# A recommender on one core: the product with W2 moves from TensorE to ScalarE, and the columns are marked anew every 16 blocks of items

## The chip, the cores and the metric

The kernel runs on one core of a Trainium2 chip. The metric is the time of one execution in device microseconds. The kernel before takes 43372.13 us in the median of three runs (43352.09 to 43403.7).

## The reference, cut to what matters

There are 50001 items with 32 neighbours each, and 16384 users with a history of 100 items and one target item.

```python
def _neighbor_attn(E, near_full):
    V = E[near_full]                                  # items x 32 x 32
    scores = einsum('nd,nkd->nk', E, V) / sqrt(32)
    return einsum('nk,nkd->nd', softmax(scores), V)

a_sus, a_inf = _neighbor_attn(E_in, near), _neighbor_attn(E_out, near)
h = concat([E_hist[history], a_sus[history], a_inf[history]])   # users x 100 x 128
t = concat([E_tgt[target], a_inf[target], a_sus[target]])       # users x 128
x = h * t[:, None, :]
z = relu(einsum('bld,hd->blh', x, W1) + b1)           # W1: 128 x 128
scores = einsum('blh,h->bl', z, W2[0])                # W2: 1 x 128
exp_A = exp(scores) * ((history != target) & (history != 0))
attn = exp_A / sqrt(sum(exp_A))
s = sum(h * attn)                                     # one number for all
pred = cosine(s * ones, t);  return sigmoid(pred)
```

## The kernel before, in words

The **item stage** builds the table of h rows (129 numbers: the sum of a row, and the row). It runs over 391 blocks of 128 items. For each block GpSimd (POOL) issues 26 indirect gathers, one for each of 26 neighbours (`gather`, L169). The other six neighbours of every item are read as columns of `cols`, a bf16 copy of the whole embedding table that stays in SBUF: `run` loads an address into a register and copies one column, 352 of the 768 by a TensorE matmul with the identity (L239), 248 by ScalarE (L235), 168 by VectorE (L237). `turn` (L264) brings the columns back into rows. VectorE then does scores, maximum, weighted sums (`scores`, `attended`), ScalarE the Exp.

The **user stage** takes 128 blocks of 128 users each; below "user" means such a block. A user has five chunks of 20 history positions, 640 chunks in all. For chunk s, POOL gathers 20 rows per user (`gather`, L534) into one of HB = 3 row buffers. VectorE (DVE) forms x = h * t (L548), copies the row sums out (`hsum`, L554) and turns x in blocks of 32 x 32 (L562) into one of XB = 2 buffers `xb`. SP writes it to DRAM in four pieces (L576) and reads it back with features on partitions (`xT`, L582). TensorE (PE) multiplies by W1 in five matmuls of 512 columns (`hidden`, L589), ScalarE (ACT) does relu over pairs of them (`relu`, L603) from two PSUM buffers. The product with W2 is again a matmul: `scored` (L613) multiplies each 128 x 512 z by `pick`, a matrix with W2 in one of 32 columns, so that the 25 matmuls of a user lay their results into 25 rows of one PSUM tile `bank`. When the 25th is done, DVE turns the bank (`weights`, `flat`, L621) and four DMAs carry it to `score`; then come Exp (L635) and the masked sums (L641 to L644).

The order is written by hand: each engine takes its instructions in the order of the loop over s. Three links matter below. The copy `hsum` of chunk s waits for the first W1 matmul of chunk s - XB (`after(copy, first.pop(s - XB))`). The gathers of chunk s wait for the `hsum` of chunk s - HB, which frees their row buffer. And `flat` stands in DVE's queue one step after the user's last chunk, ahead of the x of the next chunk. Scored matmuls run LS = 4 behind the hidden ones, in alternation with them.

Of the kernel before, what the change touches and what calls it, by code (L numbers as in the profile page):

```python
# [13 lines left out]
E = mybir.EngineType  # L14
# [36 lines left out]
W = 1 + D  # L51
M = 2
HB = 3
XB = 2
ZB = 4
LS = 4

# [8 lines left out]
Q_ACT = {6: 248}  # L66
TURN = P * NF

@with_exitstack
def kernel(
# [41 lines left out]
    with (  # L114
# [7 lines left out]
    ):  # L122
        cols = n_c.tile([P, 3, C], BF16, name="cols")
        its = {}
        subs = {}
# [85 lines left out]
        def run(s, who, q0, n):  # L211
            it, j = divmod(s, NSUB)
            u = subs[s]
            k, i = divmod(q0, P)
            k += j * NF + NF - fetched(s)
# [12 lines left out]
            for q, value in enumerate(found):  # L228
# [9 lines left out]
                else:  # L238
                    nc.tensor.matmul(pc[:, :, q : q + 1], identb, of, start=True, stop=True)  # L239

        def pieces(who, q0, q1):
# [15 lines left out]
        def turn(s):  # L257
            u = subs[s]
            fb = u.pop("fb")
            nf = fetched(s)  # L260
# [114 lines left out]
        for s in range(NT + 3):  # L375
# [11 lines left out]
            if f is not None:  # L387
                nf = fetched(f)
                subs[f]["fb"] = n_s.tile([P, 3, P * NF], BF16, name="fb", bufs=2)
# [58 lines left out]
    w1T = const.tile([D, HID], F32, name="w1T")  # L448
    pick = const.tile([HID, NG, GS], F32, name="pick")
    num = const.tile([P, UC], F32, name="num")  # L450
# [18 lines left out]

    rows = ring("h", HB, LQ, W)  # L470
    xs = ring("x", 2, LQ, D)
    xbs = ring("xb", XB, Q, LQ, GS)
    xTs = ring("xT", 3, Q * LQ * GS)
    zr = ring("z", ZB, 2, COLS)
    hists = {}
# [5 lines left out]
    with (  # L481
        tc.manual_schedule(engines={E.PE, E.Activation, E.DVE, E.SP, E.Pool}),
        tc.tile_pool(name="u_s", bufs=3) as u_s,
        tc.tile_pool(name="ps_r", bufs=2, space=bass.MemoryType.PSUM) as ps_r,
        tc.tile_pool(name="ps_t", bufs=2, space=bass.MemoryType.PSUM) as ps_t,
        tc.tile_pool(name="ps_s", bufs=2, space=bass.MemoryType.PSUM) as ps_s,
    ):
        users = {}
        landed, went, turned, moved, hid, zs = {}, {}, {}, {}, {}, {}
        bank, first, second, third = {}, {}, {}, {}  # L490

# [38 lines left out]
        def gather(s):  # L530
            c, k = divmod(s, NCH)
            for q in range(LQ):
                l = k * LQ + q
                landed[s, q] = nc.gpsimd.indirect_dma_start(  # L534
# [3 lines left out]
                    in_offset=bass.IndirectOffsetOnAxis(  # L538
                        ap=users[c]["hidx"][:, l : l + 1], axis=0
                    ),  # L540
                )

        def blocks(s):
            c, k = divmod(s, NCH)
            u = users[c]
            h = rows[s % HB]
            x = xs[s % 2]
            made = nc.vector.tensor_tensor(  # L548
                x,
                h[:, :, 1:W],  # L550
                u["tp"].to_broadcast([P, LQ, D]),
                ALU.mult,
            )
            copy = nc.vector.tensor_copy(  # L554
                u["hsum"][:, k * LQ : (k + 1) * LQ], h[:, :, 0:1].rearrange("p q o -> p (q o)")
            )
            for q in range(LQ - 1):
                gone = landed.pop((s, q))
# [3 lines left out]
            turn = nc.vector.transpose(  # L562
                xb.rearrange("p b q j -> p q b j"), x.rearrange("p q (b i) -> p q b i", b=Q)
            )
            if s >= XB:
                after(copy, first.pop(s - XB))
# [4 lines left out]

        def move(s):
            xb = turned.pop(s)
            there = theres[s % XB]
            for a in range(Q):
                one = nc.sync.dma_start(  # L576
                    there[:, :, a, :].rearrange("b i n -> i b n"),
                    xb[a * GS : (a + 1) * GS].rearrange("p b q j -> p b (q j)"),
                )
                went.setdefault(s, []).append(one)  # L580
            xT = xTs[s % 3]
            nc.sync.dma_start(xT, there.rearrange("b i a n -> (b i) (a n)"))  # L582
            moved[s] = xT

        def hidden(n):
            s, m = divmod(n, PER)
            if n % 2 == 0:
                hid[n // 2] = ps_r.tile([HID, 2, COLS], F32, name="z_ps")
            one = nc.tensor.matmul(  # L589
                hid[n // 2][:, n % 2, :],  # L590
                w1T,
                moved[s][:, m * COLS : (m + 1) * COLS],
                start=True,
                stop=True,
            )
            if m == 0:
                first[s] = one
            if m == PER - 1:
                moved.pop(s)

        def relu(pair):
            zs[pair] = zr[pair % ZB]
            second[pair] = nc.scalar.activation(zs[pair], hid.pop(pair), AF.Relu, bias=b1_sb)  # L603
            if pair >= ZB:
                covered(second[pair], second.pop(pair - ZB))
                covered(second[pair], third.pop(2 * (pair - ZB)))
                covered(second[pair], third.pop(2 * (pair - ZB) + 1))

        def scored(n):
            c, g = divmod(n, NG)  # L610
            if g == 0:
                bank[c] = ps_s.tile([GS, COLS], F32, name="bank")
            third[n] = nc.tensor.matmul(  # L613
                bank[c], pick[:, g, :], zs[n // 2][:, n % 2, :], start=g == 0, stop=g == NG - 1
            )
            if n % 2 == 1:
                zs.pop(n // 2)

        def weights(c):
            flat = u_t.tile([GS, COLS], F32, name="flat", bufs=2)  # L620
# [4 lines left out]
            of = flat[:, 0 : Q * L].rearrange("p (k a q) -> p k a q", k=NCH, a=Q)  # L625
            for a in range(Q):
                nc.sync.dma_start(
                    score[a * GS : (a + 1) * GS, :].rearrange("p (k q) -> p k q", k=NCH), of[:, :, a, :]
                )
            users[c]["score"] = score  # L630
# [15 lines left out]
        USERS = UC  # L646
        last = USERS * NCH
        groups = USERS * NG
        nc.sync.dma_start(tidx, target.rearrange("(p c) -> p c", p=P))
# [7 lines left out]
        nc.vector.tensor_copy(tidf, tidx)  # L657
        nc.vector.memset(pick, 0.0)
        for g in range(NG):
            nc.vector.tensor_copy(pick[:, g, g : g + 1], w2_sb)  # L660
# [4 lines left out]
        for s in range(last + 3):  # L665
            c, k = divmod(s, NCH)
            if s < last:
                if k == 0 and c % BSUB == 2 and 0 < c // BSUB and c // BSUB + 1 < UC // BSUB:
                    history_of(c // BSUB + 1)
# [5 lines left out]
                if k == 3 and c + 1 < USERS:  # L675
                    target_work(c + 1)
            for m in range(PER):
                n = s * PER + m
                if n < groups:
                    hidden(n)  # L680
                    if n % 2 == 1:
                        relu(n // 2)
                if 0 <= n - LS < groups:
                    scored(n - LS)
            done, left = divmod(s - NCH, NCH)
            if 0 <= done < USERS and left == 1:
                weights(done)
            if 0 <= done < USERS and left == 2:
                summed(done, ended(done))

# [78 lines left out]
```

## Time and profile before

| | |
|---|---|
| median of three runs | 43372.13 us |
| profiled execution, its span | 43228.8 us |
| span to median | 143.3 us |
| item stage | 0 to 24304 us |
| user stage | 24305 us to the end |
| busy share of the span: POOL, PE, DVE, ACT | 50%, 34%, 33%, 29% |
| DMA queues' share of 16 engines, hardware and software | 13.3%, 12.1% |

The profiled execution's own time is its span; what a run takes beside it is the 143.3 us. The busy shares are a mean over two stages. In the 40 slices of the page POOL stands at 3 to 4 tenths in the item stage and at 6 in the user stage, PE at 2 and then 4, ACT at 3 to 4 and then 0 to 1. TensorE's granted clock is full in the item stage and 6 to 7 tenths in the user stage.

### The profile page before, as it was taken

How to read it: one execution, taken by the hardware profiler on the slowest of the kernel's cores; microseconds unless marked ns; L12 is line 12 of the kernel's file. 1: busy time of each engine (PE TensorE's matmuls, PEld its weight loads, DVE VectorE, ACT ScalarE, POOL GpSimd, SP SyncE). 2: the span in 40 equal slices, each digit the busy share in tenths (PEclk: the TensorE clock that was granted, in tenths of full speed). 3: DMA queues.
4: the chain of work that ended last, by engine and by line, in shares of the span. 5: the costliest groups of instructions: out<-in, count | busy, mean ns of one | idle time of the engine just before them, and what ended most of it. 6: DMA issues, size and time to landing. Idle time of an engine off the chain costs nothing.

```text
span 43228.8 us, 542122 instructions
## 1 busy us (share of the span) xinstructions
PE 14536.1 (34%) x156212; PEld 6850.6 (16%) x156212; DVE 14230.3 (33%) x72584; ACT 12567.9 (29%) x102055; POOL 21816.3 (50%) x23124
## 2 busy tenths in 40 slices
PE   2222222222222222222222344444444444444444
PEld 1222222222222222222222100000000000000000
DVE  3444444444444444444444322222222222222222
ACT  3444444444444444444444201001010100000011
POOL 4334333343433334334343566666666666666665
PEclk9999999999999999999999867767666767677676
DMA  2000000000000000000000244444444444444444
GB/s 67 18 18 19 18 19 18 18 19 18 19 18 19 18 18 19 18 18 19 18 19 19 74 130 139 136 133 140 134 135 140 133 133 139 131 133 141 130 133 132
DMA packets 1617140, 3049.96 MB, mean 71 GB/s; under 512 B 739104, under 2 KB 831328, under 8 KB 1531840
## 3 DMA queue, kind: packets, MB, share of 16 engines
q1 hardware_dynamic: 874368, 1826.09, 13.3%
q0 software_dynamic: 739776, 1189.19, 12.1%
q8 instruction: 1238, 20.28, 0.2%
q14 instruction: 1758, 14.40, 0.1%
HBM read 2110.12 MB, written 909.58 MB: 70 GB/s over the span
## 4 chain that ended last, share of the span: by engine, by line
another core or an unknown queue 36%; issue 24%; ACT 16%; PE 9%; DVE 5%; DMA 5%; POOL 2%; ACTq 1%; SPq 1%; DVEq 0%; POOLq 0%
ACT fb L235 13%; PE pc L239 3%; PE z_ps L589 3%; DMA xT<-there 2%; POOL h L534 2%; DVE x L548 2%; PE bank L613 2%; PE rows L264 2%; DMA there<-xb 1%; ACTq L216 1%; DVE xb L562 1%; ACT z L603 1%; DVE fb L237 1%; SPq L576 1%
## 5 line engine op out<-in xcount | busy, mean ns | idle before, releaser
L169 POOL DMA_INDIRECT v<-in_egeo_dram,nidx x10190 | 9616.4, 944 | 14607.6 <-DVE tot L336 11594.1
L534 POOL DMA_INDIRECT h<-table,hidx x12800 | 12078.5, 944 | 6582.5 <-issue 3946.8
L235 ACT COPY fb<-cols 128x3 bf16 x95976 | 9824.6, 201 | 737.3 <-issue 680.8
L239 PE MATMUL pc<-cols,identb 128*128 x136224 | 5147.4, 168 | 14104.4 <-issue 13853.8
L589 PE MATMUL z_ps<-xT,w1T 128*128 128x512 f32 x6400 | 4632.4, 813 | 10706.5 <-DMA xT<-there 3875.3
L237 DVE COPY fb<-cols 128x3 bf16 x65016 | 5526.7, 167 | 4501.3 <-issue 4438.6
L239 PEld LDWEIGHTS <-identb 128*128 128x128 bf16 x136224 | 4442.4, 104 | 14783.8 <-issue 14782.3
L603 ACT ACTIVATE z<-z_ps,b_sb 128x1024 f32<-128x1024 f32 x1600 | 1775.3, 1113 | 17042.8 <-remote 7924.7
L613 PE MATMUL bank<-z,pick 128*32 128x512 f32 x6400 | 3979.7, 709 | 0.0
L275 ACT COPY v<-rows 128x384 f32<-128x384 f32 x387 | 185.0, 478 | 12603.5 <-PE rows L264 6318.7
L589 PEld LDWEIGHTS z_ps<-xT,w1T 128*128 128x128 f32 x6400 | 1208.6, 236 | 14036.0 <-issue 8731.7
L283 DVE COPY_PREDICATED v<-odd,rows 128x384 f32<-128x384 int32 x387 | 225.2, 582 | 9227.4 <-ACT v L275 9227.4
L621 DVE STREAM_TRANSPOSE flat<-bank 32x512 f32<-32x512 f32 x128 | 132.0, 1032 | 9028.3 <-remote 7940.9
L264 PE MATMUL rows<-identb,fb 128*128 128x128 bf16 x6966 | 1135.4, 297 | 3656.1 <-issue 3643.2
L548 DVE TENSOR_TENSOR x<-h,tp 128x2560 f32<-128x2560 f32 x640 | 1793.3, 2802 | 1099.1 <-DMA h<-table,hidx 650.4
L562 DVE STREAM_TRANSPOSE xb<-x 128x2560 f32<-128x2560 f32 x640 | 1819.6, 2843 | 0.0
L330 DVE TENSOR_TENSOR pw<-v,small 128x1024 f32<-128x1024 f32 x782 | 1423.1, 1900 | 46.7 <-ACT small L294 45.3
L264 PEld LDWEIGHTS <-fb 128*128 128x128 bf16 x6966 | 708.5, 132 | 4113.9 <-issue 4103.2
L641 DVE TENSOR_TENSOR ea<-ea,keep 128x100 f32<-128x100 f32 x128 | 33.6, 263 | 3543.3 <-ACT ea L635 2802.8
L613 PEld LDWEIGHTS bank<-z,pick 128*32 128x32 f32 x6400 | 478.6, 117 | 3204.1 <-issue 3202.6
L306 DVE TENSOR_REDUCE sc<-pw 128x64 f32<-128x2048 f32 x391 | 894.5, 2288 | 20.3 <-remote 6.9
L299 DVE TENSOR_TENSOR pw<-v,small 128x2048 f32<-128x2048 f32 x391 | 894.3, 2287 | 16.7 <-DVE v L283 1.9
(73 smaller groups left out, 3200.5 us busy)
## 6 DMA issues: line engine op xcount, KB each, us to landing
there<-xb SPq DMA_DIRECT2D x2560, 320.0 KB
xT<-there SPq DMA_DIRECT2D x640, 1280.0 KB
h<-table,hidx POOLq DMA_INDIRECT x12800
v<-in_egeo_dram,nidx POOLq DMA_INDIRECT x10190
table<-row SPq DMA_DIRECT2D x391, 64.5 KB
cols<-parts SPq DMA_DIRECT2D x1, 18768.0 KB
parts<-fb SPq DMA_DIRECT2D x32, 576.0 KB
own<-in_egeo_dram SPq DMA_DIRECT2D x391, 32.0 KB
```

The costliest lines, as they stand in the source:

```text
L169: nc.gpsimd.indirect_dma_start(out=v[:, k].rearrange("p t d -> p (t d)"), out_offset=None, in_=egeo, in_offset=bass.IndirectOffsetOnAxis(a ...
L235: nc.scalar.copy(to, of)
L237: nc.vector.tensor_copy(to, of)
L239: nc.tensor.matmul(pc[:, :, q : q + 1], identb, of, start=True, stop=True)
L264: nc.tensor.matmul(got[:, k].rearrange("p h d -> p (h d)"), fb[:, a, k * P : (k + 1) * P], identb, start=a == 0, stop=a == 2,)
L330: nc.vector.tensor_tensor(wv[:, t].rearrange("p d k -> p k d"), u["v"][:, :, t, :], u["sm"][:, 2 + t, :].rearrange("p (k o) -> p k o", o=1 ...
L534: landed[s, q] = nc.gpsimd.indirect_dma_start(out=rows[s % HB][:, q, :], out_offset=None, in_=table, in_offset=bass.IndirectOffsetOnAxis(a ...
L548: made = nc.vector.tensor_tensor(x, h[:, :, 1:W], u["tp"].to_broadcast([P, LQ, D]), ALU.mult,)
L562: turn = nc.vector.transpose(xb.rearrange("p b q j -> p q b j"), x.rearrange("p q (b i) -> p q b i", b=Q))
L589: one = nc.tensor.matmul(hid[n // 2][:, n % 2, :], w1T, moved[s][:, m * COLS : (m + 1) * COLS], start=True, stop=True,)
L603: second[pair] = nc.scalar.activation(zs[pair], hid.pop(pair), AF.Relu, bias=b1_sb)
L613: third[n] = nc.tensor.matmul(bank[c], pick[:, g, :], zs[n // 2][:, n % 2, :], start=g == 0, stop=g == NG - 1)
```

## The change

The user stage no longer has the `scored` matmuls, `pick`, and the turn of the bank on DVE. After the relu (now 128 x 1536 from `za` and 128 x 1024 from `zb`, one PSUM buffer each), ACT multiplies all 128 x 2560 of z by W2, one factor per partition. DVE turns that in blocks of 32 x 32 into `zT` and sums each run of 32, two chunks after the chunk itself (`partial`, LAG = 2). Once per user one matmul with `fold` adds the four quarters, and ACT copies the bank out. Rings change: row buffers 3 to 5, `xb` and the DRAM buffers 2 to 3, x 2 to 1, z from four of 1024 to three of 2560. The last user's last chunk of 20 is cut into 12 and 8. The first gather of each of the last two users waits for DVE's turn of the chunk before (CALM).

In the item stage `again` copies one column of `cols` onto itself on DVE before every 16th block, which therefore stands behind all earlier readers of `cols` and before all later ones; the identity for the column matmuls is copied anew at the same place. This happens 24 times.

```diff
+        def again(s):
+            it, j = divmod(s, NSUB)
+            _, found = nc.values_load_multi_w_load_instructions(
...
+            one = cols[:, :, ds((value - base) // 2, 1)]
+            nc.vector.tensor_copy(one, one)
...
+                if e not in idbs:
+                    again(f)
+                    idbs[e] = n_s.tile([P, P], BF16, name="idb", bufs=2)
+                    nc.vector.tensor_copy(idbs[e], ident)
...
+            if k == 0 and c >= UC - CALM:
+                after(landed[s, 0], turns[s - 1])
...
+        def hidden(s):
+            per = chunks[s][3] * P // COLS
+            xT = moved.pop(s)
+            z = zr[s % ZB]
+            for lo, hi, name in ((0, min(FIRST, per), "za"), (FIRST, per, "zb")):
...
+                z_ps = ps_r.tile([HID, PER - FIRST if lo else FIRST, COLS], F32, name=name)
+                for m in range(lo, hi):
+                    one = nc.tensor.matmul(
...
+                nc.scalar.activation(
+                    z[:, lo * COLS : hi * COLS],
+                    z_ps[:, 0 : hi - lo].rearrange("h m n -> h (m n)"),
+                    AF.Relu,
+                    bias=b1_sb,
+                )
+            nc.scalar.activation(z[:, 0 : per * COLS], z[:, 0 : per * COLS], AF.Copy, scale=w2_sb)
+
+        def partial(s):
...
+            nc.vector.transpose(
+                zT[:, 0 : Q * n].rearrange("p x i -> p (x i)"), zr[s % ZB][:, 0 : n * P]
+            )
+            nc.vector.tensor_reduce(
+                parts[c][:, :, q0 : q0 + n],
+                zT[:, 0 : Q * n].rearrange("p (a q) i -> p a q i", a=Q),
+                AX.X,
+                ALU.add,
+            )
+
+        def folded(c):
+            bank = ps_s.tile([GS, Q * L], F32, name="bank")
+            nc.tensor.matmul(
+                bank, fold, parts.pop(c).rearrange("p a l -> p (a l)"), start=True, stop=True
+            )
...
-            nc.vector.transpose(
-                flat.rearrange("p (g n) -> p n g", g=GS), bank.pop(c).rearrange("p (n j) -> p n j", j=GS)
-            )
+            nc.scalar.copy(flat.rearrange("p a l -> p (a l)"), users[c]["bank"])
```

How the order on PE changes, in the middle of the user stage. Before, a hidden matmul and a scored one alternate; names with a number are ring buffers:

```order
L613 MATMUL bank<-z_940047,pick 32x512
L589 MATMUL z_ps<-xT_940046,w1T 128x512
L613 MATMUL bank<-z_940047,pick 32x512
L589 MATMUL z_ps<-xT_940046,w1T 128x512
L613 MATMUL bank<-z_940048,pick 32x512
L589 MATMUL z_ps<-xT_940044,w1T 128x512
```

The same engine in the changed kernel, one user from fold to fold:

```order
L665 MATMUL bank<-part,fold 32x400
L633 MATMUL za<-xT_940191,w1T 128x512 x3
L633 MATMUL zb<-xT_940191,w1T 128x512 x2
L633 MATMUL za<-xT_940192,w1T 128x512 x3
L633 MATMUL zb<-xT_940192,w1T 128x512 x2
L633 MATMUL za<-xT_940190,w1T 128x512 x3
L633 MATMUL zb<-xT_940190,w1T 128x512 x2
L633 MATMUL za<-xT_940191,w1T 128x512 x3
L633 MATMUL zb<-xT_940191,w1T 128x512 x2
L633 MATMUL za<-xT_940192,w1T 128x512 x3
L633 MATMUL zb<-xT_940192,w1T 128x512 x2
L665 MATMUL bank<-part,fold 32x400
```

A user has 26 matmuls on PE where it had 50. On DVE before, around the end of a user, the turn of the bank stands between the chunks:

```order
L554 COPY hsum<-h_940038 128x20
L562 STREAM_TRANSPOSE xb_940043<-x_940041 128x20x4x32
L621 STREAM_TRANSPOSE flat<-bank 32x16x32
L548 TENSOR_TENSOR x_940040<-h_940039,tp 128x2560
L554 COPY hsum<-h_940039 128x20
L562 STREAM_TRANSPOSE xb_940042<-x_940040 128x20x4x32
L641 TENSOR_TENSOR ea<-ea,keep 128x100
```

On DVE in the changed kernel every chunk has a turn and a sum for the chunk two back:

```order
L587 COPY hsum<-h_940182 128x20
L595 STREAM_TRANSPOSE xb_940189<-x_940186 128x20x4x32
L653 STREAM_TRANSPOSE zT_940196<-z_940193 128x2560
L656 TENSOR_REDUCE part<-zT_940196 128x4x20
L581 TENSOR_TENSOR x_940186<-h_940183,tp 128x2560
L587 COPY hsum<-h_940183 128x20
L595 STREAM_TRANSPOSE xb_940187<-x_940186 128x20x4x32
```

The wait for PE's bank has gone from DVE's queue; a wait for ACT's scaled z of two chunks before stands in every chunk instead.

## Rows read from the trace of the kernel before

**Rows 1.** Head of the page.

```profile
span 43228.8 us, 542122 instructions
```

**Rows 2.** Busy time by windows, 2000 us of the user stage; first line names the columns.

```profile
core 0: us, PE busy (x) PEld busy (x) DVE busy (x) ACT busy (x) POOL busy (x), PEclk, DMA share, GB/s
34000.00:36000.00 2000.00, 872.32 (x1364) 179.24 (x1364) 427.24 (x332) 196.81 (x225) 1291.38 (x1369) 0.70 0.47 137
```

**Rows 3.** Timeline of POOL, user stage: start, duration, operation, idle time before it.

```profile
24304.95 0.94 POOL L504 DMA_INDIRECT t<-ttab,tidx  x1 [79.67 <-DMA table<-row]
...
30042.77 0.94 POOL L534 DMA_INDIRECT h<-table,hidx  x1 [14.93 <-DVE hsum L554]
30044.02 0.95 POOL L534 DMA_INDIRECT h<-table,hidx  x1 [0.30 <-issue]
...
30066.49 0.94 POOL L534 DMA_INDIRECT h<-table,hidx  x1 [0.30 <-issue]
...
30073.17 0.94 POOL L534 DMA_INDIRECT h<-table,hidx  x1 [4.49 <-DVE hsum L554]
...
43124.45 0.94 POOL L534 DMA_INDIRECT h<-table,hidx  x1 [0.30 <-issue]
```

**Rows 4.** Waits from 26000 to 42000 us: total us, times, longest.

```profile
DVE flat L621 <- remote: 6959.4, 97, 75.0
...
POOL h L534 <- DVE hsum L554: 2242.8, 201, 26.5
```

**Rows 5.** Timeline of DVE around one user's end.

```profile
30072.84 2.85 DVE L562 STREAM_TRANSPOSE xb<-x 128x2560 f32<-128x2560 f32 x1
...
30184.35 1.03 DVE L621 STREAM_TRANSPOSE flat<-bank 32x512 f32<-32x512 f32 x1 [65.75 <-remote]
```

**Rows 6.** Timeline of ACT in POOL's first long run of gathers.

```profile
24388.59 1.11 ACT L603 ACTIVATE z<-z_ps,b_sb 128x1024 f32<-128x1024 f32 x1 [7.35 <-remote]
24410.99 1.11 ACT L603 ACTIVATE z<-z_ps,b_sb 128x1024 f32<-128x1024 f32 x1 [21.29 <-remote]
...
24522.99 1.11 ACT L603 ACTIVATE z<-z_ps,b_sb 128x1024 f32<-128x1024 f32 x1 [21.29 <-remote]
24546.09 1.11 ACT L603 ACTIVATE z<-z_ps,b_sb 128x1024 f32<-128x1024 f32 x1 [21.99 <-remote]
```

**Rows 7.** Busy time by windows in the item stage, POOL idle and POOL gathering.

```profile
12014.00:12044.00 30.00, 10.19 (x300) 8.99 (x300) 18.94 (x135) 22.60 (x212) 1.17 (x2) 1.00 0.04 10
...
12056.00:12066.00 10.00, 1.00 (x6) 0.52 (x5) 0.52 (x3) 0.00 (x0) 7.56 (x9) 1.00 0.15 26
```

**Rows 8.** Timeline of POOL late in its first long run.

```profile
24540.07 1.09 POOL L534 DMA_INDIRECT h<-table,hidx  x1 [0.30 <-issue]
...
24549.87 0.94 POOL L534 DMA_INDIRECT h<-table,hidx  x1 [0.30 <-issue]
```

**Rows 9.** Costliest groups of the page: busy us, mean ns; idle before.

```profile
L589 PE MATMUL z_ps<-xT,w1T 128*128 128x512 f32 x6400 | 4632.4, 813 | 10706.5 <-DMA xT<-there 3875.3
L603 ACT ACTIVATE z<-z_ps,b_sb 128x1024 f32<-128x1024 f32 x1600 | 1775.3, 1113 | 17042.8 <-remote 7924.7
L613 PE MATMUL bank<-z,pick 128*32 128x512 f32 x6400 | 3979.7, 709 | 0.0
...
L562 DVE STREAM_TRANSPOSE xb<-x 128x2560 f32<-128x2560 f32 x640 | 1819.6, 2843 | 0.0
...
L306 DVE TENSOR_REDUCE sc<-pw 128x64 f32<-128x2048 f32 x391 | 894.5, 2288 | 20.3 <-remote 6.9
```

**Rows 10.** Timeline at the border between two item blocks.

```profile
12038.83 3.26 ACT L235 COPY fb<-cols 128x3 bf16 x32
...
12040.53 3.66 DVE L330 TENSOR_TENSOR pw<-v,small 128x1024 f32<-128x1024 f32 x2
12040.70 1.03 PE L239 MATMUL pc<-cols,identb 128*128 x32 [1.56 <-issue]
```

**Rows 11.** Timeline of the tail: SP and PE after the last chunk's turn.

```profile
43140.02 3.43 SPq L576 DMA_DIRECT2D there<-xb  x4
...
43152.78 2.08 PE L589 MATMUL z_ps<-xT,w1T 128*128 128x512 f32 x2 [7.04 <-DMA xT<-there]
```

More of the change, by code (lines that the diff above doesn't have):

```diff
@@ L51 @@
 W = 1 + D
[L52 to L56, printed above, removed]
+HB = 5
+XB = 3
+ZB = 3
+LAG = 2
+CALM = 2
+ENDING = (20, 20, 20, 20, 12, 8)
+FIRST = 3
 BF16 = mybir.dt.bfloat16
@@ L530, in gather @@
         def gather(s):
-            c, k = divmod(s, NCH)
-            for q in range(LQ):
-                l = k * LQ + q
+            c, k, q0, n = chunks[s]
+            for q in range(n):
                 landed[s, q] = nc.gpsimd.indirect_dma_start(
@@ L554, in blocks @@
             copy = nc.vector.tensor_copy(
[L555 removed]
+                u["hsum"][:, q0 : q0 + n], h[:, 0:n, 0:1].rearrange("p q o -> p (q o)")
             )
[L557 removed]
+            for q in range(n - 1):
                 gone = landed.pop((s, q))
@@ L581, in move @@
             xT = xTs[s % 3]
-            nc.sync.dma_start(xT, there.rearrange("b i a n -> (b i) (a n)"))
+            nc.sync.dma_start(
+                xT[:, 0 : Q * n * GS].rearrange("p (a n) -> p a n", a=Q),
+                there[:, :, :, 0 : n * GS].rearrange("b i a n -> (b i) a n"),
+            )
             moved[s] = xT
[L585 to L594, printed above, removed]
-            )
[L596 to L614, printed above, removed]
-            )
-            if n % 2 == 1:
-                zs.pop(n // 2)
+        def hidden(s):
[3 more added lines that the diff above has]
+            for lo, hi, name in ((0, min(FIRST, per), "za"), (FIRST, per, "zb")):
+                if hi <= lo:
+                    continue
+                z_ps = ps_r.tile([HID, PER - FIRST if lo else FIRST, COLS], F32, name=name)
+                for m in range(lo, hi):
+                    one = nc.tensor.matmul(
+                        z_ps[:, m - lo, :],
+                        w1T,
+                        xT[:, m * COLS : (m + 1) * COLS],
+                        start=True,
+                        stop=True,
+                    )
+                    first.setdefault(s, one)
+                nc.scalar.activation(
[3 more added lines that the diff above has]
+                    bias=b1_sb,
+                )
+            nc.scalar.activation(z[:, 0 : per * COLS], z[:, 0 : per * COLS], AF.Copy, scale=w2_sb)
@@ L646 @@
         USERS = UC
-        last = USERS * NCH
-        groups = USERS * NG
+        last = len(chunks)
+        closing = {s + LAG: c for s, (c, k, q0, n) in enumerate(chunks) if q0 + n == L}
         nc.sync.dma_start(tidx, target.rearrange("(p c) -> p c", p=P))
@@ L657 @@
         nc.vector.tensor_copy(tidf, tidx)
-        nc.vector.memset(pick, 0.0)
-        for g in range(NG):
-            nc.vector.tensor_copy(pick[:, g, g : g + 1], w2_sb)
+        for b in range(Q):
+            nc.vector.tensor_copy(
+                fold[b * GS : (b + 1) * GS, :], ident[b * GS : (b + 1) * GS, b * GS : (b + 1) * GS]
+            )
         w1_at = ps_t.tile([P, 1, D], F32, name="tp")
@@ L664 @@
         target_work(0)
-        for s in range(last + 3):
-            c, k = divmod(s, NCH)
+        for s in range(last + LAG + 3):
             if s < last:
+                c, k, q0, n = chunks[s]
                 if k == 0 and c % BSUB == 2 and 0 < c // BSUB and c // BSUB + 1 < UC // BSUB:
@@ L676 @@
                     target_work(c + 1)
[L677 to L689, printed above, removed]
+            if s - 1 in closing:
+                weights(closing[s - 1])
+            if s < last:
+                hidden(s)
+            if 0 <= s - LAG < last:
+                partial(s - LAG)
+                if s in closing:
+                    folded(closing[s])
+            if s - 2 in closing:
+                waiting = (closing[s - 2], ended(closing[s - 2]))
+            if s - 3 in closing:
+                summed(*waiting)
     with (
```

65 lines of the change are left out of this document (44 added, 21 removed).

## Prediction

> **What bounds the kernel now.** I read the span first [rows 1], then the kernel by stages. The item stage (24304 us) keeps its work but for `again`; so the user stage decides. Its first gather starts at 24304.95 and its last at 43124.45 us [rows 3]; with five times 20 gathers and one of targets per user that is 128 x 101 = 12928 gathers in 18820 us, 147.0 us per user. In the window of the stage POOL is the busiest engine, 1291 of 2000 us, against 872 for PE, 427 for DVE and 197 for ACT [rows 2].
>
> POOL then: from 30044.02 to 30066.49 it starts 19 gathers, 18 pitches of 1.248 us [rows 3]. A user of gathers alone is 101 x 1.248 = 126.1 us. The other 20.9 us are pauses, in each of which POOL waits for `hsum`: 14.93 and 4.49 us in the user shown [rows 3], 2242.8 us in 16000 us, or 20.6 us per user [rows 4]. Why `hsum` is late is seen on DVE: it stands 6959 us in those 16000 us before `flat` [rows 4], 65.75 us in one user [rows 5], until the last scored matmul has reported. So POOL waits for DVE, and DVE for PE.
>
> But PE is not full of work. While POOL gathers without a break, something serves PE slowly. In POOL's first long run ACT's z follow each other at exactly 22.40 us from 24388.59 to 24522.99 (six equal distances), though ACT's own work is 1.11 us [rows 6]. Between two z lie two hidden and two scored matmuls, each two records of the profile (6400 records for 3200 matmuls [rows 9]): 22.40 / 8 = 2.80 us per record, against 813 and 709 ns of their own [rows 9]. The item stage shows the same: 300 matmul records in 30 us while POOL is idle, six in 10 us late in a run of gathers [rows 7]. It is no matter of ACT or DVE, which idle there. I call this the slow service; the profile doesn't show its cause, only that it comes with POOL's runs.
>
> POOL itself is held once: in the first run, after 235 us or some 188 gathers, seven pitches from 24540.07 to 24549.87 are 1.40 us each, the instruction 1.09 instead of 0.94 us [rows 8]. I read this as a hidden queue behind the gathers, worked off at 1.40 us per gather, that POOL normally fills and that drains in the pauses.
>
> **The change, part by part.**
> Scored matmuls: 25 per user go, a fold comes; PE's records fall from 100 to 52. DVE no longer waits for the bank.
> ACT: the relu of a chunk costs 2.5 x 1.113 = 2.8 us [rows 9], as now. The product with W2 over 2560 columns is not in the trace; by the relu it is at most 2.5 x 1.113 = 2.78 us, and with a fixed part of the relu taken off no less than about 2.2; I take 2.5. Five times that adds 12.5 us per user to an engine that is busy 10% [rows 2]: hidden.
> DVE: the turn of z is the form of L562, 2.84 us; the sum of 2560 by L306, 2288 ns for 2048, is 2.86 us [rows 9]. 5.7 us per chunk, 28.5 per user, beside some 31 us now (427 of 2000 us [rows 2]): 60 of 147 us. Hidden, if what it waits for is in time. The new wait is for ACT's scaled z of two chunks before; behind it in DVE's queue stand the next chunk's x and `hsum`, for which POOL waits, but only after five row buffers instead of three. From a chunk's turn to PE's start is 43140.02 to 43152.78, 12.8 us [rows 11]; ten records at 2.80 us are 28.0, relu and scaling 3.6: 44.4 us, where two chunks of POOL at 25 us are 50. It just holds; were it late, POOL would pause, the slow service end, and PE catch up.
> PE in the slow service: 52 x 2.80 = 145.6 us per user, more than POOL's 126.1. So PE, not DVE, is what is late next if POOL never pauses.
> Does the added DVE work hold POOL? Beside the turn of xb at 30072.84 POOL's gather at 30073.17 takes its usual 0.94 us [rows 3, 5]; I add nothing. [...]
> `again`: 24 times DVE copies a column and the identity between two blocks. At such a border ACT starts the new block's columns at 12038.83, PE at 12040.70, DVE is free at 12040.53 [rows 10]; so ACT would wait about 2 us and PE less. 24 x 2 = 48 us; from 0, if hidden in later waits, to 240 us, if 10 us each.
> CALM: two users' first gather waits for the turn before, a stop of about 10 us (x and turn, 5.7 us by [rows 9], and the landing before, an estimate): 20 us. The ending in 12 and 8: now 43228.8 - 43125.4 = 103 us from the last gather to the end. The last 8 positions need a turn, 12.8 us to PE, four records, relu, scaling, sum, fold and scores; I take 50 us, from 30 to 130 (if PE is far behind).
>
> **The sum.** If POOL never stops but is held to the queue's 1.40 us, a user takes 101 x 1.40 = 141.4 us. PE at 145.6 would fall behind by 4.2 us per user, until POOL must pause a little, upon which the service quickens; so the two settle close to 141. 24304.95 + 48 + 128 x 141.4 (18099) + 20 + 50 = 42522 us, against a span of 43228.8. The run around the span is 43372.13 - 43228.8 = 143.3 us, which I leave: 42665, rounded 42670 us, 1.6% less. With 140 to 143 us per user, the spread I allow this reading, and the bounds of `again` and the tail: 42400 to 43150.
>
> **The rivals.**
> (1) POOL is free. The seven slow pitches came from something else than a full queue; without the waits for the bank POOL streams at 1.248: 24353 + 128 x 126.1 + 70 = 40564, with 143 around it 40710 us. For it: the first run went on at 1.248 for 235 us before the seven, and two more row buffers, 25 us each, outlast its present pauses of 15 and 4.5. Against it: PE's 145.6 in a run without pauses. A mixture at 131 to 139 us per user gives 41330 to 42360.
> (2) PE binds throughout at 145.6: 24353 + 18637 + 70 + 143 = 43200 us, 0.4% less. For it: 22.40 us is constant over 134 us. Against it: each pause of POOL ends it.
> (3) The gain is hidden: what paces POOL now is the draining of its own queue, whoever is named as the releaser, and a user stays at 147: 43390 us with `again` and the shorter tail. For it: 147.0 is only 5.6 above 141.4.
> (4) Slower. The slow service grows further in longer runs. It has done so in the run shown up to 2.80 us per record, and the last distance is 23.10 us [rows 6], 2.89 per record. From 147.0 / 52 = 2.83 us per record on, the new user is longer than the old. At 2.89 it is 150.3 us: 24353 + 19238 + 70 + 143 = 43800 us; at 3.5, 47700. For it: the change makes POOL's runs longer, as DVE stops it less. Against it: six distances of the same 22.40 before, and POOL's row buffers run out when PE lags.
>
> **How the numbers follow.** The forecast has 0.45, (1) with its mixtures 0.22, (2) 0.13, (3) 0.08, (4) 0.12. The predicted time is the forecast's, 42670 us. For 8 in 10 the range leaves out the free POOL below 41300 (about 0.1) and slower than 43450 (about 0.1). A measurement of this kernel tells 0.2% (87 us) from no change: faster holds the forecast, (1) and (2), 0.80; within 0.2%, mostly (3), 0.07; slower, (4) and a rest of (3), 0.13.
>
> **What would show it.** Right: POOL's gathers mostly in runs of some hundreds with pitches of 1.40 us, or of 1.248 with pauses of together about 15 us per user; no wait of DVE over 20 us; z in steps of 16.8 and 11.2 us (six and four records at 2.80); the item stage at 24304 plus 0 to 100 us. Wrong in the hidden queue: a long run at 1.248 throughout. Wrong in PE: records under 2 us in POOL's runs. Wrong altogether: pauses of POOL still near 21 us per user, or DVE standing before the turn of z as long as before `flat`.

## The result, and the profile after

The changed kernel takes 42686.48 us in the median of four runs (42636.35 to 42706.82), the kernel before 43362.92 us (43352.09 to 43403.7, four runs): a ratio of 0.9841, 95% interval 0.9827 to 0.9854. Predicted were 42670 us. The profiled execution has a span of 42704.9 us, its own time being 42706.82 us.

The page's head and the window of the user stage, answering to [rows 1, 2], with a window of 3500 us early in the stage between them:

```profile
span 42704.9 us, 531495 instructions
...
25000.00:28500.00 3500.00, 1035.53 (x1248) 350.71 (x1248) 1409.79 (x798) 637.45 (x480) 2669.79 (x2500) 0.60 0.48 139
...
34000.00:36000.00 2000.00, 606.99 (x739) 207.87 (x737) 824.06 (x467) 375.26 (x282) 1394.93 (x1424) 0.60 0.47 140
```

POOL issues 1424 gathers in the 2000 us where it issued 1369: 141.9 us per user of 101 gathers. PE has 739 matmul records instead of 1364; DVE is busy 824 us instead of 427, ACT 375 instead of 197. The work that was added is there, and it lies beside the gathers.

POOL's timeline, answering to [rows 3, 8]: the first gather of the stage, a piece of the first long run, the start of a user after a pause, the starts of the last two users, the last gather.

```profile
24513.07 0.95 POOL L536 DMA_INDIRECT t<-ttab,tidx  x1 [81.44 <-DMA ttab<-row]
...
26003.28 1.10 POOL L565 DMA_INDIRECT h<-table,hidx  x1 [0.31 <-issue]
26004.68 1.10 POOL L565 DMA_INDIRECT h<-table,hidx  x1 [0.30 <-issue]
...
34832.22 0.94 POOL L565 DMA_INDIRECT h<-table,hidx  x1 [17.88 <-DVE hsum L587]
34833.47 0.94 POOL L565 DMA_INDIRECT h<-table,hidx  x1 [0.31 <-issue]
...
42385.74 0.94 POOL L565 DMA_INDIRECT h<-table,hidx  x1 [65.32 <-DVE xb L595]
...
42519.03 0.94 POOL L565 DMA_INDIRECT h<-table,hidx  x1 [7.52 <-DVE xb L595]
...
42642.59 0.95 POOL L565 DMA_INDIRECT h<-table,hidx  x1 [0.30 <-issue]
```

From 24513.07 to 42643.54 there are 12928 gathers, 1.402 us each: 141.6 us per user. The mean hides two regimes. In the first, of which 26003.28 is a piece, POOL never pauses for about 4200 us. From 25000 to 28500 us it issues 2500 gathers, 1.400 us each in the mean; the single pitches are mixed, many still 1.25 us and others 1.40 us and more, the held instruction taking some 1.10 instead of 0.94 us. In the second regime it runs mostly at 1.25 us and pauses once per user, here for 17.88 us, for `hsum`. The pauses of 65.32 and 7.52 us are those that CALM sets.

The waits from 26000 to 42000 us (total us, times, longest), answering to [rows 4]. The wait before the turn of z has two rows, one for each thing that the profile names as having ended it:

```profile
ACT z L641 <- remote: 8495.1, 727, 17.0
DVE zT L653 <- ACT z L647: 4203.8, 267, 23.7
DVE zT L653 <- issue: 2806.3, 172, 23.1
POOL h L565 <- DVE hsum L587: 1019.0, 76, 20.7
```

The wait for `flat` is gone; DVE now stands before the turn of z, 7010 us of 16000 by the two rows, at most 23.7 us at a time. Before `flat` it stood 7758 us over all rows of that wait (6959 in the row of [rows 4]), up to 75 us at a time. So DVE waits nearly as long as before, but in short pieces, and POOL's pauses have fallen from 2243 to 1019 us.

What still makes POOL pause is seen on DVE just before the pause that ends at 34832.22:

```profile
34828.00 0.26 DVE L687 TENSOR_TENSOR ea<-ea,keep 128x100 f32<-128x100 f32 x1 [21.09 <-ACT ea L681]
...
34831.78 0.17 DVE L587 COPY hsum<-h 128x20 f32<-128x20 f32 x1
```

In 75 of the 76 pauses of over 1 us in these 16000 us, DVE's last wait ahead of the awaited `hsum` is this one: the masked sums of a user stand in its queue and wait for ACT's Exp (L681).

ACT's timeline in one user, answering to [rows 6]; `za` is the relu of three matmuls, `zb` that of two:

```profile
34142.28 1.54 ACT L641 ACTIVATE z<-za,b_sb 128x1536 f32<-128x1536 f32 x1 [13.23 <-remote]
34152.78 1.11 ACT L641 ACTIVATE z<-zb,b_sb 128x1024 f32<-128x1024 f32 x1 [8.96 <-remote]
...
34170.28 1.54 ACT L641 ACTIVATE z<-za,b_sb 128x1536 f32<-128x1536 f32 x1 [13.93 <-issue]
```

From one `za` to the next are 28.00 us: ten records at 2.80 us in the mean, as before the change. Singly the records don't come at that distance. In POOL's first long run PE does the six of `za` in 5.04 us and the four of `zb` in 3.78 us, and waits in between:

```profile
26005.30 5.04 PE L633 MATMUL za<-xT,w1T 128*128 128x512 f32 x6 [15.25 <-ACT z L641]
26015.37 3.78 PE L633 MATMUL zb<-xT,w1T 128*128 128x512 f32 x4 [5.04 <-issue]
```

The item stage is longer. The sums of scores (391 of them) and the window of the stage, of the kernel before and then of the changed one; the last start stands behind "to", the granted clock behind the engines:

```profile
L306 DVE TENSOR_REDUCE sc<-pw x391: 2279/2287/2290, 220.2 to 24292.5; 128x64 f32<-128x2048 f32 x196
...
0.00:24304.00 24304.00, 6314.20 (x143410) 5162.90 (x143410) 10258.80 (x69501) 10703.71 (x99937) 9617.07 (x10196) 1.00 0.10 21
```

```profile
L327 DVE TENSOR_REDUCE sc<-pw x391: 2277/2287/2291, 219.9 to 24500.6; 128x64 f32<-128x2048 f32 x196
...
0.00:24304.00 24304.00, 6190.62 (x142009) 5064.57 (x142009) 10296.17 (x68833) 10674.11 (x98994) 9564.97 (x10143) 0.50 0.09 20
```

208 us are added over 390 steps from block to block. Averaged by place within 16 blocks, from the starts of these sums, every step is about 0.46 us longer (62.16 against 61.70 us without the borders), and the one at the border with `again` another 1.33 us. So `again` accounts for 24 x 1.33 = 32 us, and some 176 us lie on every block. In this execution TensorE's granted clock is 0.50 through the whole stage, where it was 1.00 before. That the clock makes the 0.46 us is not shown, and the times speak against it as the whole cause: the other three runs of the changed kernel have a mean clock of 0.83 instead of 0.54 and are 15 to 70 us faster, not 176, and the kernel before, on another chip with a mean clock of 0.586, took 43157.75 us, no more than here. Part of the 176 us may belong to the pair of executions that was traced: the two traces lie 524 us apart, the two medians 676 us, as the traced execution of the kernel before was a quick one.

The tail, answering to [rows 11]:

```profile
42673.02 1.76 SPq L612 DMA_DIRECT2D there<-xb  x4
...
42680.85 3.44 PE L633 MATMUL za<-xT,w1T 128*128 128x512 f32 x4 [16.23 <-DMA xT<-there]
...
42702.07 0.36 SPq L759 DMA_DIRECT2D out_dram<-res  x1
```

From the last gather's end to the end of the span are 61.4 us, where there were 103.

### The profile page after: what moved, and what is told of

The parts are those of the page before. It is cut to its first block, busy times and chain, and to the rows that moved or that the text cites. A ratio compares the mean times of both kernels' runs of the same rounds, so it can differ in the third digit from the quotient of the medians.

```text
span 42704.9 us, 531495 instructions
## 1 busy us (share of the span) xinstructions
PE 11681.9 (27%) x150068; PEld 6977.0 (16%) x150068; DVE 17859.6 (42%) x73767; ACT 14179.0 (33%) x102504; POOL 22525.2 (53%) x23124
## 4 chain that ended last, share of the span: by engine, by line
issue 21%; another core or an unknown queue 18%; ACT 7%; POOL 4%; PE 4%; DVE 3%; SPq 1%; DMA 1%; ACTq 0%; DVEq 0%; POOLq 0%
POOL h L565 4%; ACT fb L240 4%; ACT z L641 2%; PE pc L244 1%; PE za L633 1%; PE zb L633 1%; SPq L612 1%; DVE x L581 1%; DVE xb L595 1%; DVE part L656 1%; DVE zT L653 1%; PE rows L285 0%; DMA xT<-there 0%; ACT z L647 0%
## 5 line engine op out<-in xcount | busy, mean ns | idle before, releaser
L244 PE MATMUL pc<-cols,idb 128*128 x132000 | 4881.7, 168 | 13100.9 <-issue 12925.2
L244 PEld LDWEIGHTS <-idb 128*128 128x128 bf16 x132000 | 4248.0, 104 | 13583.5 <-issue 13550.5
L633 PE MATMUL za<-xT,w1T 128*128 128x512 f32 x3844 | 3191.4, 998 | 10129.3 <-issue 3706.7
L653 DVE STREAM_TRANSPOSE zT<-z 128x2560 f32<-128x2560 f32 x641 | 1814.3, 2830 | 7395.5 <-ACT z L647 4465.3
L641 ACT ACTIVATE z<-za,b_sb 128x1536 f32<-128x1536 f32 x641 | 986.9, 1540 | 8741.3 <-remote 6102.5
L633 PEld LDWEIGHTS za<-xT,w1T 128*128 128x128 f32 x3844 | 1153.7, 320 | 12229.5 <-issue 8538.2
L633 PE MATMUL zb<-xT,w1T 128*128 128x512 f32 x2556 | 2115.4, 975 | 2630.2 <-issue 1797.7
L285 PE MATMUL rows<-idb,fb 128*128 128x128 bf16 x6750 | 1128.9, 296 | 4266.4 <-issue 4257.7
L656 DVE TENSOR_REDUCE part<-zT 128x80 f32<-128x2560 f32 x641 | 1804.9, 2816 | 21.9
L647 ACT ACTIVATE z<-z,w_sb 128x2560 f32<-128x2560 f32 x641 | 1554.1, 2424 | 21.0
```

The source lines that it names most:

```text
L285: nc.tensor.matmul(got[:, k].rearrange("p h d -> p (h d)"), fb[:, a, k * P : (k + 1) * P], identb, start=a == 0, stop=a == 2,)
L633: one = nc.tensor.matmul(z_ps[:, m - lo, :], w1T, xT[:, m * COLS : (m + 1) * COLS], start=True, stop=True,)
L641: nc.scalar.activation(z[:, lo * COLS : hi * COLS], z_ps[:, 0 : hi - lo].rearrange("h m n -> h (m n)"), AF.Relu, bias=b1_sb,)
L653: nc.vector.transpose(zT[:, 0 : Q * n].rearrange("p x i -> p (x i)"), zr[s % ZB][:, 0 : n * P])
L656: nc.vector.tensor_reduce(parts[c][:, :, q0 : q0 + n], zT[:, 0 : Q * n].rearrange("p (a q) i -> p a q i", a=Q), AX.X, ALU.add,)
```

## The experiments

What had to be tested is the slow service, since everything follows from it. The reading of the prediction is called theory Q below: gathers pass through a hidden queue that takes 1.40 us for each, and while it is filled the other engines are served slowly. Most programs leave out the item stage and fill the tables with zeros, so that the user stage stands alone:

```diff
-        for s in range(NT + 3):
...
+    zero = const.tile([P, NSUB * W], F32, name="zero")
+    nc.vector.memset(zero, 0.0)
+    for i in range(NITER):
+        nc.sync.dma_start(table.rearrange("(i p j) d -> i p (j d)", p=P, j=NSUB)[i], zero)
+        nc.sync.dma_start(ttab.rearrange("(i p j) d -> i p (j d)", p=P, j=NSUB)[i], zero[:, 0 : NSUB * D])
```

**Gathers beside one engine at a time.** The edit: no kernel at all, but phases, parted by pauses.

```diff
+PHASES = (("g", 800), ("b", 300), ("f", 300), ("A", 300), ("V", 300), ("half", 500), ("thin", 500), ("g", 60))
+STREAM = {"b": 500, "f": 250, "A": 1500, "V": 1500}   # matmuls bf16, fp32; copies on ScalarE, VectorE
```

> A small program that leaves out the whole computation (its output is zeros) and runs, in phases parted by about 70 us of idle gathers: 800 gathers of 128 rows x 516 bytes alone; 300 gathers beside 500 small bf16 matmuls; 300 beside 250 fp32 matmuls of 512 columns; 300 beside 1500 small ScalarE copies; 300 beside 1500 small VectorE copies; 500 gathers of 64 rows; 500 gathers of 128 rows x 256 bytes. Theory Q (a hidden queue behind the gathers, worked off at 1.40 us per gather, and TensorE served slowly beside it): in the first phase the pitch is 1.248 us for some 190 gathers and 1.40 from then on, 800 gathers in about 1090 us; matmul records come at 2.8 us each after some 30 us of gathers; ScalarE and VectorE copies keep 0.1 to 0.25 us each. If the cost of 1.40 goes by the rows, 64 rows show no held pitch; if it goes by the instruction, they show the same. Rival F (POOL is free, the seven slow pitches were an accident of other transfers): 1.248 throughout, 800 gathers in 999 us. Rival P (TensorE's slowness comes from the transfers of the user stage, not from the gathers): matmul records stay under 1.2 us here.

Measured: 1.248 us per gather in every phase, 800 of them included (1.204 us with 64 rows), and 500 matmuls in 13.5 us: no slow service. But beside it the kernel before took 28991.94 us. So the condition under which the prediction's trace was taken was not there at all, and an execution of the same kernel without it takes two thirds of the time.

> The same small program as before (it leaves out the whole computation), beside another run of the kernel before. The first look showed no slow service at all, 1.248 us per gather throughout and matmuls at their own speed, and in the same job the kernel before took 28992 us and not 43363. So theory S: the slow service is not a property of the program alone; it is there in some executions and not in others, and where it is there it makes 43.4 ms of 29.0. Expected: if the kernel before takes 43.3 to 43.5 ms here, the first 800 gathers take about 1090 us (1.40 each after some 190) and the 500 small matmuls come at about 2.8 us each; if it takes 29 ms, everything is as in the first look. Rival P (the slowness comes from the transfers of the user stage): no slow matmuls in this program, whatever the kernel before takes.

On another chip the same: 4456.91 us, the kernel before 28990.94 us. Neither run could test theory Q. Beside the 43362.92 us of the result they show that the same kernel takes 29.0 or 43.4 ms.

**The two user stages, and the whole changed kernel, without the slow service.**

> The user stage of the kernel before alone: the item stage is left out and the table of h rows is zeros. Theory Q: where the kernel before takes 43.4 ms, this takes 18.9 ms (its stage in the trace) plus some 0.2 ms to fill the tables, 147 us per user, with POOL's two pauses per user. Where the kernel before takes 29 ms, POOL's gathers alone bound it: 128 x 126.1 = 16.1 ms plus 0.3. Rival (DVE's wait for the bank bounds it by itself): 18.9 ms in both.

> The user stage of the changed kernel alone, with the same parts left out. Theory Q: where the kernel before takes 43.4 ms, 128 x 141.6 = 18.1 ms plus 0.3, 0.957 of the stage before; where it takes 29 ms, 16.1 ms plus 0.3, the same as the stage before within 1%. Rival (the change saves work that bounds in any case): the ratio is below 0.97 in both.

Measured 16322.86 us (the stage before) and 16324.99 us (the changed one), beside a kernel before at 28990.94. From 4000 to 14000 us POOL gathers without a single pause in both (no wait over 0.3 us, 1603 and 1602 gathers in 2000 us, 1.248 us each); CALM sets two at the end of the changed stage. POOL's longest waits in the changed stage between 4000 and 14000 us:

```profile
POOL h L214 <- issue: 2365.5, 7762, 0.3
POOL h L214 <- DMA h<-table,hidx: 51.8, 170, 0.3
```

> The changed kernel once more, whole, beside the kernel before, to see it under whichever of the two conditions this execution has. Theory S with Q: if the kernel before takes 43.3 to 43.5 ms, this takes 42.64 to 42.71 and the ratio is 0.984. If the kernel before takes 29.0 ms, POOL's gathers bound both stages and both kernels: 391 x 26 x 1.248 = 12.69 ms and 16.14 ms; the change adds only its 24 column copies (about 1.4 us each, 33 us) and a shorter tail (some 40 us less), ratio 0.999 to 1.002. Rival (the change saves work of its own): 0.98 in both.

Measured 28995.52 us against 28991.23: ratio 1.0002, interval 0.999 to 1.0013. Without the slow service the change is worth nothing; the rival that it saves work which bounds in any case has fallen. The trace of this run also shows where the slow service costs most. Its sums of scores, to be set beside the changed kernel's row of 219.9 to 24500.6 above:

```profile
L327 DVE TENSOR_REDUCE sc<-pw x391: 2277/2287/2291, 139.5 to 12785.2; 128x64 f32<-128x2048 f32 x196
```

A block of items takes 32.4 us here and 62.3 us there, so that some 11.6 of the 13.7 ms between the changed kernel's two times lie in the item stage.

**A pause at every user, and a fifth fewer gathers.** The edits in the changed stage:

```diff
-CALM = 2
+CALM = UC - 1
```

```diff
+        def got_of(s):
+            n = chunks[s][3]
+            return n if s < HB else n * 4 // 5
...
-            for q in range(n):
+            for q in range(got_of(s)):
```

> The changed user stage alone (item stage left out, tables zero), with the first gather of every user but the first waiting for the turn of the chunk before, so that POOL pauses once per user. Without the slow service POOL's gathers bound the stage and every pause is paid: about 8 us x 127 = 1.0 ms on 16.32, 17.3 ms. With the slow service theory Q says that the pauses only drain the hidden queue that has to be drained anyway: the same 18.1 to 18.3 ms as without them; the rival that POOL's own time and its pauses just add up says 18.1 + 1.0 = 19.1.

> The changed user stage alone (item stage left out, tables zero), with 16 of the 20 gathers of every chunk from the sixth on: the other four rows keep what an earlier chunk left. Without the slow service: 81 x 1.248 = 101.1 us per user, 12.94 ms plus 0.2, 13.15 ms. With it theory Q: POOL's part falls to 81 x 1.40 = 113.4 us, TensorE's stays at 145.6 while POOL runs, so between: 120 to 135 us per user, 15.4 to 17.3 ms. If TensorE alone bound it there: 18.6 ms; if the hidden queue alone: 14.5 ms.

Measured 17241.85 and 13165.51 us, beside a kernel before at 28991.23: again without the slow service. The stage has 125 pauses more than the changed one; they cost 917 us, 7.3 each, and four gathers less per chunk bring 3159 us. There POOL's gathers are all that bounds.

**The end and the rings.** The edits, each in the changed stage:

```diff
-CALM = 2
-ENDING = (20, 20, 20, 20, 12, 8)
+CALM = 0
+ENDING = (20, 20, 20, 20, 20)
```

```diff
-HB = 5
-XB = 3
+HB = 3
+XB = 2
```

> The changed user stage alone (item stage left out, tables zero), without the two pauses at the end and with the last chunk of 20 whole. Against the same stage with them (16325.0 us where POOL bounds): the prediction priced the two pauses at 20 us and the shorter tail at some 50 of 103 us. So by it 16325 - 20 + 20 to 30: between 16315 and 16345 us; if the pauses cost what they took in the stage with a pause per user (917 us / 126 = 7.3 us each), 16310 plus what a chunk of 20 needs more than one of 8 at the end (12 gathers less to wait are no gain; x, turn, matmuls and sums are some 10 us longer): 16320.

> The changed user stage alone (item stage left out, tables zero) with the old rings: three row buffers and two of xb. Where POOL bounds (the kernel before at 29 ms): no difference, 16325 us within 10. Where the slow service is there: POOL can run ahead by three chunks less, so the time in which TensorE is behind reaches POOL sooner; theory Q says the mean is set by the hidden queue and TensorE alike and expects 18.1 to 18.4 ms; the rival that the rings make the gain expects 18.8 to 18.9 ms.

Measured 16319.01 us (16318.85 to 16319.68) and 16326.35 us, without the slow service. The plain end is 6 us faster than the changed one: its last gather starts at 16264.45 instead of 16280.89, so that the two pauses cost 16.4 us, and what follows takes 51.7 instead of 42.0, so that the ending in 12 and 8 saves 9.7 us. What the rings are worth under the slow service was not measured. What the two pauses are worth there no run singles out, but the changed kernel's trace shows them: POOL stood 65.32 and 7.52 us. At the first it had run ahead, and the turn that it waited for stood behind four other chunks in DVE's queue.

**Phases, pauses and doubled matmuls in one program.** The phases of the small program (those beside the copies cut to 150 gathers and 800 copies), then the changed stage for 96 users with a pause at every user, then for 96 users with every hidden matmul issued twice:

```diff
+STAGES = ((NU - 1, 0, 0), (2, 1, 0))        # pauses, doubled matmuls, fewer gathers
...
-                    one = nc.tensor.matmul(
+                        for again_ in range(1 + twice):
+                            one = nc.tensor.matmul(
```

> One program of several parts, the item stage left out and the tables zero: first the phases of the small program (800 gathers alone; 300 beside small matmuls; 300 beside fp32 matmuls; copies on ScalarE and VectorE; gathers of 64 rows and of 256 bytes), then the changed user stage for 96 users with POOL's pause at every user, then the changed stage for 96 users with every hidden matmul issued twice (104 matmul records more per user than the change has). Where the kernel before takes 29 ms: all gathers at 1.248 us; 96 x 126.1 + 95 x 7.2 = 12.8 ms for the stage with pauses; 96 x 126.1 = 12.1 ms for the doubled one, if TensorE stays below 126 us per user (50 fp32 matmuls took 977 of 2000 us in the stage before). Where it takes 43.4 ms, theory Q: 1.40 us per gather after some 190, small matmuls 2.8 us each, 13.6 ms with the pauses (141.6 per user) and 14.1 to 14.8 ms doubled (147 to 154 per user, as in the kernel before, which has as many records); rival (pauses add to a slow POOL): 14.3 ms with the pauses; rival (TensorE binds at 2.8 us per record without end): 27 ms doubled.

> The program of several parts once more (item stage left out, tables zero), on another chip, to meet the slow service if it depends on the chip. Where the kernel before takes 29 ms: 28645 us as before. Where it takes 43.4 ms, theory Q: 1.40 us per gather after some 190 gathers alone, small matmuls 2.8 us each beside gathers, 141.6 us per user with a pause at every user, and 147 to 154 with every hidden matmul twice; rivals as in the first run of this program.

The first run, beside a kernel before at 28990.34 us, took 28644.9 us. The second ran on a fifth chip, beside a kernel before at 43157.75 us: the slow service was there, and the program took 32288.51 us. These two runs of one program tell what it does. Windows of the first: 500 small matmuls beside gathers, ScalarE copies beside gathers, the stage with pauses, the stage with doubled matmuls (columns as in [rows 2]):

```profile
1197.00:1220.00 23.00, 13.71 (x500) 13.56 (x500) 0.09 (x1) 0.00 (x0) 17.16 (x19) 1.00 0.24 51
2093.00:2213.00 120.00, 0.00 (x0) 0.00 (x0) 0.33 (x1) 102.95 (x528) 90.45 (x96) 0.50 0.25 53
...
12000.00:14000.00 2000.00, 518.50 (x780) 202.48 (x780) 870.48 (x495) 396.93 (x300) 1428.71 (x1515) 0.63 0.53 149
20000.00:22000.00 2000.00, 891.79 (x1618) 366.46 (x1619) 916.39 (x519) 417.81 (x314) 1511.81 (x1603) 0.70 0.56 158
```

The same of the second, with the slow service:

```profile
1340.00:1380.00 40.00, 2.30 (x14) 1.57 (x15) 0.00 (x0) 0.00 (x0) 30.25 (x33) 1.00 0.24 53
2280.00:2400.00 120.00, 43.45 (x43) 12.30 (x43) 0.00 (x0) 16.77 (x86) 90.64 (x97) 0.50 0.25 53
...
12000.00:14000.00 2000.00, 597.33 (x734) 204.37 (x734) 815.32 (x462) 373.36 (x281) 1346.37 (x1421) 0.60 0.50 141
20000.00:22000.00 2000.00, 768.77 (x1368) 310.43 (x1366) 771.92 (x438) 349.01 (x263) 1260.51 (x1336) 0.68 0.46 133
```

Its 800 gathers with no other engine at work, around the place where POOL is held first, and the last:

```profile
126.58 0.94 POOL L458 DMA_INDIRECT h<-table,hidx  x1 [0.30 <-issue]
...
358.75 0.94 POOL L458 DMA_INDIRECT h<-table,hidx  x1 [0.30 <-issue]
359.99 1.04 POOL L458 DMA_INDIRECT h<-table,hidx  x1 [0.30 <-issue]
361.34 1.09 POOL L458 DMA_INDIRECT h<-table,hidx  x1 [0.31 <-issue]
...
1215.34 1.09 POOL L458 DMA_INDIRECT h<-table,hidx  x1 [0.31 <-issue]
```

POOL runs at 1.248 us until 359.99, some 188 gathers, and then at (1215.34 - 361.34) / 610 = 1.400 us to the end; 1091 us for 800, as theory Q said. Gathers of 64 rows (22 starts from 3249.98 to 3279.39) and of 256 bytes (8 starts from 3734.41 to 3744.21) are held at the same 1.40 us: in these phases the cost goes by the instruction, not by rows or bytes. Matmuls beside gathers, in the same run:

```profile
1501.34 0.16 PE L472 MATMUL accb<-small,identb 128*128 128x3 bf16 x1 [2.64 <-issue]
1504.14 0.16 PE L472 MATMUL accb<-small,identb 128*128 128x3 bf16 x1 [2.64 <-issue]
```

One record in 2.80 us for a matmul of three columns; for the fp32 matmuls of 512 columns it is 2.80 us too (nine starts from 1900.14 to 1922.54). Rival P, that the transfers of the user stage cause it, has fallen. One part of theory Q has fallen too: ScalarE is not spared. Its copies, 0.20 us long and 528 in 120 us without the slow service, come at 86 in 120 us with it:

```profile
2385.02 0.20 ACT L478 COPY small<-small 128x3 bf16<-128x3 bf16 x1 [1.21 <-ACT small L478]
2386.42 0.20 ACT L478 COPY small<-small 128x3 bf16<-128x3 bf16 x1 [1.21 <-ACT small L478]
```

1.40 us per instruction; VectorE's copies likewise, 93 in the 130 us from 2540 to 2670, 1.40 us apart. On TensorE the trace has a load of the weights for every matmul (43 of each in the window from 2280 to 2400), so 2.80 us is the same 1.40 per instruction. It looks as if, while gathers are out, each engine got one instruction through per gather worked off; by what means is not shown.

The stage with pauses makes 1421 gathers in 2000 us with the slow service, 142.2 us per user, and 1433 from 8000 to 10000 us, 141.0; at the mean of the two, 141.6, its 96 users are 13.6 ms, an estimate. Without the slow service it makes 1515, 133.3 us per user. So a pause of POOL costs 7.2 us where POOL alone bounds, and nothing against the 141.6 us of the changed kernel where the hidden queue has to drain anyway: theory Q's 13.6 ms, not the rival's 14.3. In these two windows a gather takes 1.402 us (4000 us for 2854), so that the queue's pace is all that the stage takes. (The stage with two pauses was not run beside it; the 141.6 us are those of the result's trace.) With doubled matmuls, 102 records per user, it is 1336 gathers, 151 us per user (1319 from 28000 to 30000 us, 153 each), against 1603 and 126 without. That is near the 147 us of the kernel before with its 100 records, and far from 102 x 2.80 = 286 us: TensorE catches up in POOL's pauses, as Q said; that its records set how long these must be is argued and not shown. (The expectation of the first run speaks of 104 records more; it is 50.)

## Why the prediction was right, and where it was not

*What bounds: POOL held by a queue behind the gathers, and TensorE served slowly.* Right, and shown: gathers alone are held at 1.400 us after some 188, and the changed kernel's 12928 gathers take 1.402 us each. At 1.400 us they would take 18099 us; the changed kernel's took 18130 us, the kernel before's 18820 us. So by this reading the change took away nearly all the time in which the queue stood empty, an estimate. The pace was read from seven pitches in one place [rows 8].

*A user at 141.4 us.* Right in the mean, 141.6. The way there was not "close to 141" all along. For the first 30 users POOL runs through and TensorE falls behind into the row buffers; then TensorE at 52 x 2.80 = 145.6 us per user paces several users (34832.22 is the start of one, and starts 145 us apart surround it), the queue, by theory Q, drains in pauses of up to 22 us, TensorE catches up, and POOL runs through again for two to six users. Rival (2) is thus true of stretches, and not of the stage.

*ACT and DVE hidden.* Right in time, DVE at 824 of 2000 us. The relu took 1.54 us for 1536 columns and 1.11 for 1024, by which some 0.26 us of it are the fixed part that the prediction took off, an estimate. The scaling took 2.42 us (2.5 said), the sum over 2560 took 2.82 (2.86 said). The prediction named PE as "what is late next", and it reaches DVE twice: DVE stands before zT for 7010 of 16000 us, and once per user before `ea`, for Exp, which nearly every pause of POOL follows. The prediction had no term for that second wait.

*`again`.* 48 us were said; the border steps show 32. The item stage nevertheless grew by 208 us from trace to trace, some 176 of them spread over all blocks. That term was not foreseen, and the runs don't settle it.

*CALM 20 us, tail 50.* The tail was 61.4 us. The two pauses cost 16.4 us where POOL bounds, but POOL stood 72.8 us in them under the slow service, 65.32 in the first. How much of that the stage lost is not shown, since TensorE and DVE caught up meanwhile: DVE began a chunk every 11 to 12 us instead of every 28.

*The 143.3 us around the span.* Wrong. A run's own time is its span plus 2 us (42706.82 to 42704.9); the 143 us were the distance of one quick execution of the kernel before from the median of others. The sum for the span, 42522, missed the profiled span by 183 us: 160 in the item stage, 11 in the users, 11 in the tail. The 143 us and those 183 nearly cancel, so the 16 us between 42670 and 42686 are closer than the working deserves. The term that carried the change, the users' 18099 us with 20 for the pauses, measured 18130.

*The rivals.* (1), POOL free, gave 40710 us and did not come, but only because the slow service was there; without it POOL is free in both kernels, and the change makes no difference. (3) and (4) did not come: POOL's pauses halved, and the service stayed at 2.80 us per record in the mean in a run of 4200 us. (The price of (4) at 3.5 us leaves out the 143 us that the other sums have; nothing hangs on it.)

*The signs.* The kind of gathers came as said, runs of hundreds at 1.40 us in the mean and then 1.25 us with pauses, of together 9 us per user where some 15 were said. Other signs failed though the time was right. DVE waited up to 23.7 us where no wait over 20 was to come. The z came in steps of 10.50 and 17.50 us, not 11.2 and 16.8, with the foretold sum of 28. The item stage grew by more than 100 us. "Records under 2 us" was to mean that PE was read wrongly, and most records lie 0.85 us apart within their group; only the mean is 2.80 us, as it was before. And DVE's total wait before the turn of z came close to that before `flat`, which was to mean "wrong altogether". So that sign was badly chosen: the length of the single wait tells, not the total.

What stays open is where the slow service comes from. It was absent on four chips and present on a fifth and in the runs of the prediction; whether it goes with the chip, or with what else ran there, wasn't tried. No experiment under it undid single parts of the change, so the share of the fewer records, of DVE's freed queue and of the rings in the 1.6% is argued from the traces and not separated.

## What to carry to other kernels

When an engine's instructions are short and yet come at one exact distance (2.80, 22.40, 28.00 us), look for what is served at that distance before looking for the semaphore that is named; the pauses of a third engine may be what the bound consists of. A wait that is removed pays only as far as what stands behind it: here the wait for the bank was the visible end of a queue, and the gain was 1.6% of the whole, where the pauses had been 14% of POOL's time in the user stage. And time the kernel before beside every experiment: here 28.99 against 43.16 ms for one program decided which expectation applied.

## What the runs showed of the hardware that was not expected

The same kernel took 28991 us on four chips and 43158 us on a fifth, and a gather instruction that nothing holds takes 0.94 us under either condition. Under the slow service a gather instruction, of 128 or 64 rows, of 516 or 256 bytes, took 1.400 us within a long row of them (among 800 of 128 rows and 516 bytes after some 188), and beside the gathers TensorE, ScalarE and VectorE each got one instruction through in 1.40 us in the mean (a load and a matmul in 2.80 us, 86 copies in 120 us, 93 in 130).
